# Four-layer cross-attention on one core: in layer 2, values kept in their heads' own columns and multiplied by Wo a tile later, in place of a folded V·Wo

## Chip, cores and metric

The kernel runs on one core of a Trainium2 chip. The metric is the device time of one execution in microseconds (us). Before the change three runs gave 2443.85, 2446.23 and 2447.73 us, a median of 2446.23 us.

## What is computed

The input `x` is [4, 1024, 256] in float32 and passes four attention layers, each against the same context of 77 rows a batch; every layer has 16 heads. The change concerns layer 2. Cut to its core, the reference computes there

```
q = (x @ Wq.T + bq)    k = (ctx @ Wk.T + bk)    v = (ctx @ Wv.T + bv)      # 16 heads of 16 columns
scores = q @ k.T / 4 * attention_weights ; masked to -inf
p   = softmax(scores)                                                      # [4, 16, 1024, 77]
out = (p @ v, heads side by side: [1024, 256]) @ Wo.T + bo
x   = layernorm(x + out) * gamma + beta
```

For a tile of 128 rows of `x` the weights `p` are 16 heads times 77 keys, 1232 numbers a row. The two products after the softmax can be done in either order: `(p @ v) @ Wo`, or `p @ (v @ Wo)` with `v @ Wo` worked out once for each head and batch.

## The kernel before

**Stages.** Layer 0 runs in 16 steps (4 batches of 4 "quads" of heads), then layer 1 in 16 more, then layer 2 and layer 3, each over 32 tiles of 128 rows. Layer 0 takes about the first 900 us, layer 1 ends near 1834, layer 2 has its scores from 1843 to 2097, and layer 3 runs to the end.

**How work is ordered.** The order on each engine is that in which the program issues instructions; every engine works its own queue in order, and semaphores join them. A `step` of layer 0 goes through bursts of score matmuls (line 502). After each burst, `gap` (line 472) and `fill` (line 483) issue pieces of side jobs: a `Job` (line 444) has a number of pieces, a stretch of the step in which they fall due, and, for `fill`, a cost in us (`us=`). All DMAs are issued by SyncE (SP), in program order, and all land through one queue.

**The first quad (0, 0)**, at about 40 to 113 us, has no softmax work yet: 11 bursts of scores for maxima (`Max0`, line 611), each followed by reductions on VectorE (`mpart`, line 650). Its jobs (lines 1588 to 1596) are values of layer 0, contexts, the values, folded values and keys of layer 2, and the statistics of the next batch. Before burst 6 the rows of K reach `qk` by four DMAs (`spread`, line 375); after them come the 13 DMAs that fill `qk` for the next quad.

**Folded values.** `values2` (line 931) makes v turned, with two copies of which each keeps every second head (`hsel2`). `folded2` (line 981) goes through `folded` (line 959) in 24 pieces; each multiplies a head pair's v by its rows of Wo into two PSUM tiles `pu` (128 rows by 256), copies both with ScalarE (line 920) to a staging place, and writes them with DMAs (line 974) to `kept_u[0]` in DRAM, as rows (head, key) of 256. `folded3` does the same later for layer 3, into `kept_u[1]`. `keys2` (line 945) shares the staging places.

**A slot of layer 2** (`slot2`, line 1403) works on several tiles at once. For slot i:

- ScalarE: 16 exponentials, one a head, of tile i-1 (line 1419);
- TensorE: scores of tile i into two PSUM pairs `ps`; VectorE: product with `fside` (line 1431, twice), masking (line 1436), later the maxima `nm` (line 1448, 1452);
- `gap2`: pieces of jobs (the next batch's queries `prep2`, line 1373; the layer norm of the batch before, `norm2`, line 1470);
- TensorE: `po` of tile i-4 (line 1444), ten matmuls over chunks of 128 (head, key) rows, the turned weights `pT` stationary and `U` (128 x 256) moving; VectorE adds it to `x` (line 1458), GpSimd adds `bo`;
- TensorE: the weights of tile i-3 turned in three groups of four, four and two chunks (`turned`, line 1332), each copied by ScalarE (line 1339) into `pT`;
- `gap2` again; then VectorE sums the exponentials of tile i-1 (line 1464, 1465), and GpSimd divides (line 1466).

`load_folded` (line 1354) brings `U` of a batch in two DMAs. The PSUM pool `sm` has three buffers, used in turn by the turned groups, by `prep2` and by nearly every other small product; `pv` has one. After the 32 slots, four more slots without new scores finish the lag, each set ahead of a slot of layer 3 (line 1725, 1772).

Of the kernel before, what the change touches and what calls it, by code (L numbers as in the profile page):

```python
# [17 lines left out]
P = 128  # L18
# [13 lines left out]
def tile_xattn_seq(ctx: ExitStack, tc: tile.TileContext, d: dict, out: bass.AP):  # L32
# [128 lines left out]
    row_tile("be2", "r4", d["L0_xattn_be2"])  # L161
    row_tile("b2", "r5", d["L0_xattn_b2"])

    ctn = work.tile([S, NB - 1, D], F32, name="ctn", tag="hT", bufs=3)
    nc.sync.dma_start(out=ctn, in_=d["ctx_1024"][1:NB].rearrange("b s e -> s b e"))
    load_cols_of(("L2_xattn_bv", 2), ("L2_xattn_bk", 2))
    l2 = {}
    w2s = wpool.tile([P, 3, 2, D], F32, name="w2s", tag="s3")
    for i, key in enumerate(("L2_Wv_t", "L2_Wo_t", "L2_Wk_t")):
        l2[key[3:5]] = w2s[:, i]  # L170
        load_plain(w2s[:, i], d[key])
# [43 lines left out]


    hsel = work.tile([P, HH], F32, name="hsel", tag="hsel", bufs=1)
    hsel2 = work.tile([P, 2], F32, name="hsel2", tag="hsel2", bufs=1)
    hsel4 = work.tile([P, 4], F32, name="hsel4", tag="hsel4", bufs=1)
# [24 lines left out]
    def head_masks():  # L244

        nc.gpsimd.memset(hsel, 1.0)
        nc.gpsimd.affine_select(
            out=hsel, in_=hsel, compare_op=ALU.is_ge, fill=0.0, base=0,
            pattern=[[-DH, HH]], channel_multiplier=1,
        )  # L250
        nc.gpsimd.affine_select(
            out=hsel, in_=hsel, compare_op=ALU.is_ge, fill=0.0, base=DH - 1,
            pattern=[[DH, HH]], channel_multiplier=-1,
        )
        nc.vector.tensor_reduce(
            hsel2, hsel.rearrange("p (r e) -> p e r", e=2), axis=AX.X, op=ALU.add
        )
# [673 lines left out]
    def values2():  # L931

        vb = shared["v2"] = []
        for o in range(2):
            pk = of_contexts(l2["Wv"], o)
            v = work.tile([P, 2, NS], F32, name="v2", tag="hT", bufs=3)
            for e in range(2):
                nc.vector.tensor_scalar(
                    v[:, e, :], pk, cols["L2_xattn_bv"][:, o : o + 1], hsel2[:, e : e + 1],
                    ALU.add, ALU.mult,  # L940
                )
            vb.append(v)
            yield
# [36 lines left out]

    def folded2():

        pairs = []
        for o in range(2):
            for r in (0, 2):
                for e in range(2):
                    h = HH * o + 2 * r + e
                    two = [slice(HP * (r + k), HP * (r + k) + HP) for k in range(2)]
                    pairs.append((
                        slice(h, h + 3, 2), [shared["v2"][o][q, e, :] for q in two],  # L990
                        [l2["Wo"][q, o, :] for q in two],
                    ))
        yield from folded(kept_u[0], pairs, True)

    def heads3(key):
# [25 lines left out]
    def folded3():  # L1021

        two = [slice(0, 64), slice(64, P)]
        yield from folded(
            kept_u[1],
            [
                (slice(2 * f, 2 * f + 2), [shared["wv"][f // 3][r, f % 3, :] for r in two],
                 [l3["wo"][r, f, :] for r in two])
                for f in range(8)
            ],  # L1030
            False,
        )
# [314 lines left out]
    def load2():  # L1347
        l2["Wq"] = wpool.tile([P, 2, D], F32, name="w2q", tag="s3")
        load_plain(l2["Wq"], d["L2_Wq_t"])
        row_tile("bo", "r2", d["L2_xattn_bo"])  # L1350
        row_tile("gamma", "r3", d["L2_xattn_gamma"])
        row_tile("beta", "r4", d["L2_xattn_beta"])

    def load_folded(i, b):

        U = late.tile([P, NC, D], F32, name=f"U{i + 2}", tag="qu")
        rows_of_u = kept_u[i][b].rearrange("h s n -> (h s) n")
        n = P * (NC - 1)
        nc.sync.dma_start(
            out=U[:, 0 : NC - 1, :], in_=rows_of_u[0:n].rearrange("(c p) n -> p c n", p=P)  # L1360
        )
        nc.sync.dma_start(out=U[0:HSIZE, NC - 1, :], in_=rows_of_u[n:HK])
        return U

    def loads2(b):

        shared["u2", b] = load_folded(0, b)
        yield
# [34 lines left out]
    def slot2(i, tiles, at, gap2):  # L1403


        p1, p3, p4 = tiles.get(i - 1), tiles.get(i - 3), tiles.get(i - 4)
        a = None
# [12 lines left out]
        if a:  # L1420
# [81 lines left out]
    def loads3(b):  # L1502

        G = late.tile([P, 2, 8, 2, S], F32, name="G3", tag="gs")
        nc.sync.dma_start(
            out=G.rearrange("p c f e s -> p (c f e) s"),
            in_=kept_g.rearrange("p c f e (b s) -> p (c f e) b s", s=S)[:, :, b, :],
        )
        shared["b3", b] = (G.rearrange("p c f e s -> p c (f e s)"), load_folded(1, b))
        yield  # L1510
# [69 lines left out]
    def jobs0(b, quad):  # L1580
# [222 lines left out]
```

## Time and profile before

| | |
|---|---|
| median of three runs | 2446.23 us (2443.85 to 2447.73) |
| the profiled execution: its own time, its span | 2442.25 us, 2440.5 us |
| mean granted TensorE clock | 0.974 of full speed |
| busy share of the span | TensorE 93%, VectorE 57%, ScalarE 43%, GpSimd 26% |
| first quad: first burst, next quad's first maxima | 39.9 us, 114.8 us |
| layer 2: scores of tile 4, scores of tile 31 | 1870.3 us, 2095.5 us (27 slots of 8.34 us in the mean) |

A row of the profile names line, engine, operation, the written and the read tile (their numbers left out) and the shape as partitions by elements. A float32 matmul is recorded as two instructions, so ten matmuls stand as "x20". Their recorded spans overlap by about 0.16 us, since they are pipelined: the pace of a row is the time between starts. PE is TensorE, PEld its weight loads, DVE is VectorE, ACT ScalarE, POOL GpSimd, SPq the queue of SyncE that issues DMAs.

### The profile page before, as it was taken

What the parts mean: (1) busy time and instruction counts of PE and PEld (TensorE: products, weight loads), DVE (VectorE), ACT (ScalarE), POOL (GpSimd) and SP (SyncE); (2) the same over time, 40 slices, a digit from 0 to 9 for tenths busy, and PEclk for the clock granted to TensorE, in tenths of its full rate; (3) what the DMA queues carried; (4) which work ended last, traced back from release to release, by engine and by line L of the source; (5) the groups of instructions that cost most, each with busy time, mean ns of one, the idle gap of its engine ahead of it and who ended that gap; (6) DMA issues with size and microseconds to landing.
All of it is one profiled execution on the core that took longest, in us unless ns stands there. A gap on an engine that the chain in (4) does not pass through costs nothing.

```text
span 2440.5 us, 40648 instructions
## 1 busy us (share of the span) xinstructions
PE 2279.2 (93%) x16578; PEld 1418.9 (58%) x16578; DVE 1402.0 (57%) x2365; ACT 1040.1 (43%) x1748; POOL 639.8 (26%) x923
## 2 busy tenths in 40 slices
PE   5799989899998999899999999999998999999999
PEld 3443534454454545444556666666655777788887
DVE  4446556555566545664346435454437899767664
ACT  2244444344443344444443444444445677532222
POOL 2011013111131111311152223333332356552222
PEclk9799999999999999999999999999998999999999
DMA  6412021101000000100000100101104334022200
GB/s 176 119 27 93 6 74 40 47 2 19 2 6 15 6 15 1 20 22 5 14 15 5 19 21 15 19 15 19 19 1 166 119 119 134 25 55 55 55 14 18
DMA packets 87139, 98.54 MB, mean 40 GB/s; under 512 B 31222, under 2 KB 77866, under 8 KB 86826
## 3 DMA queue, kind: packets, MB, share of 16 engines
q1 hardware_dynamic: 86954, 95.95, 14.6%
q8 instruction: 131, 2.15, 0.4%
q14 instruction: 54, 0.44, 0.1%
HBM read 57.70 MB, written 20.59 MB: 32 GB/s over the span
## 4 chain that ended last, share of the span: by engine, by line
PE 79%; DVE 10%; ACT 6%; issue 2%; POOL 2%; DMA 1%; SPq 1%; ACTq 0%; DVEq 0%; POOLq 0%
PE ps L51 33%; PE po L51 16%; PE pp L51 6%; PE pv L51 5%; DVE mpart L650 5%; PE ph L51 4%; PE ppv L51 2%; PE psT L1338 2%; PE pvw L51 2%; PE ptx L345 2%; PE pvl L51 1%; PE pk L51 1%; PE pt L591 1%; PE pu L51 1%; PE pm L574 1%
## 5 line engine op out<-in xcount | busy, mean ns | idle before, releaser
L51 PE MATMUL ps<-qk 32*128 32x192 f32 (+8 forms) x5760 | 608.2, 464 | 76.5 <-DVE mpart L650 22.1
L715 ACT ACTIVATE pe<-ps 128x1024 f32<-128x1024 f32 (+2 forms) x384 | 362.9, 951 | 596.6 <-PE ps L51 588.9
L650 DVE TENSOR_REDUCE mpart<-ps 128x2 f32<-128x1024 f32 (+3 forms) x448 | 409.4, 934 | 344.8 <-PE ps L51 344.0
L51 PEld LDWEIGHTS ps<-qk 32*128 32x128 f32 (+1 forms) x5760 | 287.4, 184 | 328.8 <-issue 97.5
L51 PE MATMUL po<-U,pT 128*128 128x256 f32 (+1 forms) x1280 | 291.9, 384 | 7.4 <-DVE x L1458 4.7
L718 POOL TENSOR_SCALAR_AFFINE_SELECT pe<-pe 128x256 f32<-128x256 f32 (+1 forms) x192 | 94.8, 494 | 698.1 <-ACT pe L715 697.1
L51 PEld LDWEIGHTS po<-U,pT 128*128 128x128 f32 (+1 forms) x1280 | 241.1, 192 | 50.1 <-ACT pT L1339 8.0
L1109 DVE TENSOR_REDUCE mrow<-ps 128x4 f32<-128x768 f32 x128 | 122.6, 958 | 142.8 <-PE ps L51 142.4
L1339 ACT COPY pT<-psT 128x512 f32<-128x512 f32 (+1 forms) x192 | 92.0, 518 | 227.9 <-PE psT L1338 227.8
L1184 ACT ACTIVATE pew<-ps 128x768 f32<-128x768 f32 x128 | 103.3, 810 | 173.2 <-PE ps L51 172.7
L1189 POOL TENSOR_SCALAR_AFFINE_SELECT pew<-pew 128x512 f32<-128x512 f32 x128 | 81.3, 635 | 344.1 <-ACT pew L1184 344.1
L51 PE MATMUL pv<-pe,va 128*32 128x512 f32 (+3 forms) x1536 | 159.8, 504 | 0.0
L51 PE MATMUL ps<-G,xT 128*128 128x308 f32 x512 | 143.0, 423 | 0.0
L1419 ACT ACTIVATE s<-s,nm 128x77 f32<-128x77 f32 x512 | 131.3, 354 | 15.9 <-DVE nm L1452 15.9
L51 PE MATMUL ph<-yT,w 128*128 128x256 f32 x512 | 133.7, 398 | 0.8 <-DVE qk L576 0.8
L1551 POOL TENSOR_TENSOR s<-s,den 128x1232 f32<-128x1232 f32 x32 | 71.9, 2248 | 207.8 <-DVE den L1550 184.8
L51 PE MATMUL po<-w,hT 128*128 128x128 f32 (+1 forms) x800 | 124.6, 310 | 0.0
L51 PEld LDWEIGHTS po<-w,hT 128*128 128x128 f32 x800 | 110.0, 193 | 20.4 <-issue 13.8
L51 PEld LDWEIGHTS ph<-yT,w 128*128 128x128 f32 x512 | 94.1, 197 | 38.6 <-issue 24.5
L51 PEld LDWEIGHTS ps<-G,xT 128*128 128x128 f32 x512 | 92.6, 190 | 26.7
L576 DVE TENSOR_TENSOR qk<-pm,qk 128x512 f32<-128x512 f32 x64 | 44.1, 689 | 105.3 <-PE pm L574 105.3
L51 PEld LDWEIGHTS <-identb 128*128 128x128 bf16 x576 | 33.1, 97 | 104.4 <-issue 100.3
(191 smaller groups left out, 3250.6 us busy)
## 6 DMA issues: line engine op xcount, KB each, us to landing
side<-in_fside_t SPq DMA_DIRECT2D x32, 616.0 KB
qk<-st SPq DMA_DIRECT2D x256, 64.0 KB
U<-kept_u SPq DMA_DIRECT2D x8, 1152.0 KB
side<-in_mask_t SPq DMA_DIRECT2D x32, 154.0 KB
G<-kept_g SPq DMA_DIRECT2D x4, 1232.0 KB
x<-in_x SPq DMA_DIRECT2D x8, 512.0 KB
out<-x SPq DMA_DIRECT2D x32, 128.0 KB
kept_u<-st SPq DMA_DIRECT2D x22, 154.0 KB
```

The costliest lines, as they stand in the source:

```text
L51: nc.tensor.matmul(o, lhsT, rhs, start=start, stop=stop, **kw)
L345: nc.tensor.transpose(pt[:, i, :], xn[i][:, c * P : (c + 1) * P], ident)
L650: nc.vector.tensor_reduce(mpart[bl][:, i, 2 * p : 2 * p + 2, ci], ps[:, :, o : o + w], axis=AX.X, op=ALU.max,)
L715: nc.scalar.activation(pp[:n, :, o:512], ps[:n, :, o:512], AF.Exp, scale=SC)
L718: nc.gpsimd.affine_select(out=own, in_=own, compare_op=ALU.is_ge, fill=0.0, base=0, pattern=[[0, 2], [0, k], [1, P]], channel_multiplier=-1,)
L1109: nc.vector.tensor_reduce(mo, ps.rearrange("p j (i n) -> p j i n", i=2)[:, :, :, 0 : P + WIN], axis=AX.X, op=ALU.max, negate=True,)
L1184: nc.scalar.activation(pp[:, :, :, 0 : P + WIN], ps.rearrange("p j (i n) -> p j i n", i=2)[:, :, :, 0 : P + WIN], AF.Exp, scale=SC,)
L1189: nc.gpsimd.affine_select(out=pf[:, :, 0:P], in_=pf[:, :, 0:P], compare_op=ALU.is_ge, fill=0.0, base=0, pattern=[[0, 4], [1, P]], channel_ ...
L1338: nc.tensor.transpose(ps[:, k, :], s[:, P * c : P * c + P], ident)
L1339: nc.scalar.copy(pT[:, 4 * group : 4 * group + n, :], ps[:, 0:n, :])
L1419: nc.scalar.activation(hs, hs, AF.Exp, bias=p1["nm"][:, h : h + 1], scale=SC)
L1551: nc.gpsimd.tensor_tensor(s3, s3, den.unsqueeze(2).to_broadcast([P, H, S]), ALU.mult)
```

## The change

Layer 2's values are no longer folded with Wo. `values2` first writes zeros over a DRAM buffer `kept_v`, then makes v of each batch untransposed (77 x 256, four products), adds the bias row, and writes each half of eight heads by one DMA: head j's row for a key is a row of 128 numbers with v in columns 16j to 16j+15 and zeros elsewhere. `folded2` and `hsel2` are gone. A batch's values come back as 11 chunks `V` of 128 rows by 128 columns, five for the first eight heads and six for the last eight (the fifth and the sixth go with the same chunk of weights), by five DMAs and one memset. In a slot, `V` is stationary and the turned weights move past it (11 matmuls with 128 moving columns), which gives the tile's attention output turned; ScalarE copies it to `oT`; one slot later two matmuls with 256 moving columns multiply it by Wo. The lag goes from four slots to five. The bias row takes the place of `b2`, which is loaded later; Wo is loaded at layer 1 beside Wq.

```diff
-    row_tile("b2", "r5", d["L0_xattn_b2"])
+    row_tile("bv2", "r5", d["L2_xattn_bv"])
...
-    w2s = wpool.tile([P, 3, 2, D], F32, name="w2s", tag="s3")
-    for i, key in enumerate(("L2_Wv_t", "L2_Wo_t", "L2_Wk_t")):
+    w2s = wpool.tile([P, 2, 2, D], F32, name="w2s", tag="s3")
+    for i, key in enumerate(("L2_Wv_t", "L2_Wk_t")):
...
     def load_w2():
+        row_tile("b2", "r5", d["L0_xattn_b2"])
...
     def values2():
-        vb = shared["v2"] = []
-        for o in range(2):
-            pk = of_contexts(l2["Wv"], o)
-            v = work.tile([P, 2, NS], F32, name="v2", tag="hT", bufs=3)
-            for e in range(2):
-                nc.vector.tensor_scalar(
-                    v[:, e, :], pk, cols["L2_xattn_bv"][:, o : o + 1], hsel2[:, e : e + 1],
-                    ALU.add, ALU.mult,
-                )
-            vb.append(v)
-            yield
+        n = NB * 2 * HH * DIAG // P // 8
+        nc.gpsimd.memset(stg[:, 0:n], 0.0)
+        nc.sync.dma_start(
+            out=kept_v.rearrange("b e x -> (b e x)").rearrange("(p k n) -> p k n", p=P, n=n),
+            in_=stg[:, 0:n].unsqueeze(1).to_broadcast([P, 8, n]),
+        )
+        yield
+        for b in range(NB):
+            pk = sm.tile([S, D], F32, name="pk", tag="sm")
+            for c in range(2):
+                mm(pk, ctxT[:, b, c, :], l2["Wv"][:, c, :], start=(c == 0), stop=(c == 1))
+            v = place(3, NS)[:S, 0:D]
+            nc.vector.tensor_tensor(v, pk, rows["bv2"][:S], ALU.add)
+            for e in range(2):
+                to = kept_v[b, e].rearrange("(j x) -> j x", x=DIAG)[:, 0 : S * P]
+                nc.sync.dma_start(
+                    out=to.rearrange("j (s p) -> s j p", p=P)[:, :, 0:DH],
+                    in_=v[:, P * e : P * e + P].rearrange("s (j r) -> s j r", r=DH),
+                )
+            yield
...
-    def folded2():
...
     def load2():
-        l2["Wq"] = wpool.tile([P, 2, D], F32, name="w2q", tag="s3")
-        load_plain(l2["Wq"], d["L2_Wq_t"])
+        w = wpool.tile([P, 2, 2, D], F32, name="w2q", tag="s3")
+        for i, key in enumerate(("L2_Wq_t", "L2_Wo_t")):
+            l2[key[3:5]] = w[:, i]
+            load_plain(w[:, i], d[key])
...
     def loads2(b):
-        shared["u2", b] = load_folded(0, b)
+        V = late.tile([P, NC, D], F32, name="V2", tag="qu").rearrange("p c n -> p (c n)")
+        V = V[:, 0 : (NC + 1) * P].rearrange("p (c n) -> p c n", n=P)
+        lo, hi = [kept_v[b, e, 0:HALF].rearrange("(r n) -> r n", n=P) for e in range(2)]
+        k = HH * S % P
+        nc.gpsimd.memset(V[:, 4:6, :], 0.0)
...
+        shared["v2", b] = V
         yield
...
     def slot2(i, tiles, at, gap2):
-        p1, p3, p4 = tiles.get(i - 1), tiles.get(i - 3), tiles.get(i - 4)
+        p1, p3, p4, p5 = (tiles.get(i - k) for k in (1, 3, 4, 5))
...
+        if p5:
+            xt = xs[p5["b"]][:, p5["t"], :]
+            po = pvp.tile([P, D], F32, name="po2", tag="pv")
+            for o in range(2):
+                mm(po, p5["oT"][:, o, :], l2["Wo"][:, o, :], start=(o == 0), stop=(o == 1))
+            del tiles[i - 5]
         if p4:
-            U = shared["u2", p4["b"]]
-            xt = xs[p4["b"]][:, p4["t"], :]
-            po = pvp.tile([P, D], F32, name="po2", tag="pv")
-            for c in range(NC):
+            V = shared["v2", p4["b"]]
+            pv = sm.tile([P, 2, P], F32, name="pvT", tag="sm")
+            for k in range(NC + 1):
+                o, c = (0, k) if k < 5 else (1, k - 1)
                 r = slice(0, rows_in(c))
-                mm(po, p4["pT"][r, c, :], U[r, c, :], start=(c == 0), stop=(c == NC - 1))
-            del tiles[i - 4]
+                mm(pv[:, o, :], V[r, k, :], p4["pT"][r, c, :], start=k in (0, 5), stop=k in (4, NC))
+            oT = p4["oT"] = late.tile([P, 2, P], F32, name="oT", tag="oT")
+            nc.scalar.copy(oT, pv)
...
-        if p4:
+        if p5:
             nc.vector.tensor_tensor(xt, po, xt, ALU.add)
             nc.gpsimd.tensor_tensor(xt, xt, rows["bo"], ALU.add)
...
-            j.append(Job(values2(), 2, 0.1, 0.2, us=1.0))
-            j.append(Job(folded2(), 24, 0.2, 1.0, us=0.85))
+            j.append(Job(values2(), 5, 0.3, 0.9, us=0.85))
...
-            j.append(Job(norm2(NB - 1), 16, 0.1, 1.0))
+            j.append(Job(norm2(NB - 1), 16, 0.15, 1.0))
...
-    run(slots(slot3, 2, jobs3, slots(slot2, 4, jobs2)))
+    run(slots(slot3, 2, jobs3, slots(slot2, 5, jobs2)))
```

More of the change, by code (lines that the diff above doesn't have):

```diff
@@ L161, in tile_xattn_seq @@
     row_tile("be2", "r4", d["L0_xattn_be2"])
-    row_tile("b2", "r5", d["L0_xattn_b2"])
+    row_tile("bv2", "r5", d["L2_xattn_bv"])
     ctn = work.tile([S, NB - 1, D], F32, name="ctn", tag="hT", bufs=3)
     nc.sync.dma_start(out=ctn, in_=d["ctx_1024"][1:NB].rearrange("b s e -> s b e"))
-    load_cols_of(("L2_xattn_bv", 2), ("L2_xattn_bk", 2))
+    load_cols_of(("L2_xattn_bk", 2))
     l2 = {}
-    w2s = wpool.tile([P, 3, 2, D], F32, name="w2s", tag="s3")
-    for i, key in enumerate(("L2_Wv_t", "L2_Wo_t", "L2_Wk_t")):
+    w2s = wpool.tile([P, 2, 2, D], F32, name="w2s", tag="s3")
+    for i, key in enumerate(("L2_Wv_t", "L2_Wk_t")):
         l2[key[3:5]] = w2s[:, i]
@@ L217, in tile_xattn_seq @@
     hsel = work.tile([P, HH], F32, name="hsel", tag="hsel", bufs=1)
-    hsel2 = work.tile([P, 2], F32, name="hsel2", tag="hsel2", bufs=1)
     hsel4 = work.tile([P, 4], F32, name="hsel4", tag="hsel4", bufs=1)
@@ L253, in head_masks @@
             pattern=[[DH, HH]], channel_multiplier=-1,
-        )
-        nc.vector.tensor_reduce(
-            hsel2, hsel.rearrange("p (r e) -> p e r", e=2), axis=AX.X, op=ALU.add
         )
@@ L900, in tile_xattn_seq @@
     kept_g = dram.tile([P, 2, 8, 2, NS], F32, name="kept_g")
-    kept_u = [dram.tile([NB, H, S, D], F32, name=f"kept_u{i}") for i in range(2)]
+    kept_u = dram.tile([NB, H, S, D], F32, name="kept_u")
+    HALF, DIAG = HH * S * P, S * P + DH
+    kept_v = dram.tile([NB, 2, HH * DIAG], F32, name="kept_v")
     stg = wpool.tile([P, 1024], F32, name="stg", tag="s7")
@@ L979, in folded @@
                 yield
-    def folded2():
-        pairs = []
-        for o in range(2):
-            for r in (0, 2):
-                for e in range(2):
[L987 to L993, printed above, removed]
     def heads3(key):
@@ L1024, in folded3 @@
         yield from folded(
-            kept_u[1],
+            kept_u,
             [
@@ L1352, in load2, with load_folded @@
         row_tile("beta", "r4", d["L2_xattn_beta"])
-    def load_folded(i, b):
-        U = late.tile([P, NC, D], F32, name=f"U{i + 2}", tag="qu")
-        rows_of_u = kept_u[i][b].rearrange("h s n -> (h s) n")
+    def load_folded(b):
+        U = late.tile([P, NC, D], F32, name="U3", tag="qu")
+        rows_of_u = kept_u[b].rearrange("h s n -> (h s) n")
         n = P * (NC - 1)
@@ L1365, in loads2 @@
     def loads2(b):
-        shared["u2", b] = load_folded(0, b)
+        V = late.tile([P, NC, D], F32, name="V2", tag="qu").rearrange("p c n -> p (c n)")
[3 more added lines that the diff above has]
+        nc.gpsimd.memset(V[:, 4:6, :], 0.0)
+        nc.sync.dma_start(
+            out=V[:, 0:4, :], in_=lo[0 : 4 * P].rearrange("(c p) n -> p c n", p=P)
+        )
+        nc.sync.dma_start(out=V[0:k, 4, :], in_=lo[4 * P :])
+        nc.sync.dma_start(out=V[k:P, 5, :], in_=hi[0 : P - k])
+        nc.sync.dma_start(
+            out=V[:, 6:10, :], in_=hi[P - k : 5 * P - k].rearrange("(c p) n -> p c n", p=P)
+        )
+        nc.sync.dma_start(out=V[0:HSIZE, 10, :], in_=hi[5 * P - k :])
+        shared["v2", b] = V
         yield
@@ L1508, in loads3 @@
         )
-        shared["b3", b] = (G.rearrange("p c f e s -> p c (f e s)"), load_folded(1, b))
+        shared["b3", b] = (G.rearrange("p c f e s -> p c (f e s)"), load_folded(b))
         yield
```

## The prediction

> **What bounds the kernel now.** I read the busy time by stage first, because the page's shares mix stages with different limits. Columns: window, length, busy us (instructions) of PE, PEld, DVE, ACT, POOL, then granted clock, DMA share, GB/s.
>
> ```profile
> 70.00:80.00 10.00, 3.36 (x18) 1.47 (x16) 0.60 (x1) 0.65 (x2) 0.00 (x0) 0.73 0.44 104
> 80.00:90.00 10.00, 5.33 (x20) 3.60 (x20) 5.45 (x8) 1.97 (x7) 0.00 (x0) 0.50 0.42 124
> ```
>
> ```profile
> 1870.00:1946.00 76.00, 75.61 (x385) 56.21 (x386) 64.71 (x88) 51.86 (x178) 27.46 (x27) 1.00 0.34 112
> 1946.00:1975.00 29.00, 27.74 (x156) 22.46 (x156) 27.18 (x36) 25.35 (x85) 22.81 (x30) 1.00 0.31 101
> 1975.00:2012.00 37.00, 36.70 (x184) 26.40 (x182) 32.73 (x49) 23.50 (x81) 15.04 (x15) 1.00 0.38 128
> 2012.00:2034.00 22.00, 21.01 (x119) 17.03 (x120) 20.86 (x29) 18.15 (x61) 15.79 (x21) 1.00 0.29 92
> 2034.00:2103.00 69.00, 60.62 (x320) 47.94 (x316) 64.88 (x108) 48.23 (x164) 42.48 (x51) 0.95 0.37 111
> ```
>
> Two places matter. In the first quad no engine is busy between 70 and 90 us; something else is waited for. In layer 2 TensorE is full at first, but VectorE stands at 85% to 95% throughout: work taken from TensorE is worth only what VectorE leaves. The chain of waits (start, length, what) says what is late in the first quad:
>
> ```profile
> 71.85 0.48 SPq L974
> 72.33 0.06 issue
> 72.44 0.31 SPq L974
> 72.75 0.05 issue
> 72.80 4.03 DMA kept_u<-st
> ...
> 79.86 4.05 DMA kept_k<-st
> 84.06 0.38 ACT st L920
> 84.48 1.06 PE pu L51 x2
> ```
>
> SP first issues the next quad's `qk` DMAs (62 to 72 us); `folded2`'s writes stand behind them, its staging places stay taken, ScalarE cannot copy `pu`, and TensorE stands. The group of `pu` has the size:
>
> ```profile
> L51 PE MATMUL pu<-w2s,v 32*128 32x256 f32 x96 | 26.7, 530 | 15.0 <-ACT st L920 12.4 <-DVE wfd L1058 1.6 <-ACT stg L920 0.9
> ```
>
> So 26.7 us busy and 15.0 us of TensorE idle hang on `folded2`, in a quad of 75 us (39.9 to 114.8).
>
> **First quad, part by part.** *Removed:* 96 `pu` records, 48 ScalarE copies of 0.37 us, the `kept_u` writes of layer 2, and the turned values. *Added:* a zero fill, 16 records of 77 x 256 (four of this shape take 1.02 us, row `pvc`: 4 us in all), four VectorE additions of 0.42 us, eight DMAs.
>
> Up to the K rows' arrival: the chain holds 2.1 us of turned values and about 5.5 us of `pu` and copies between 45 and 61 us. VectorE's reductions, two of 1.1 us a burst, cover part, so I take 5 us: K lands at 58.5 in place of 63.5.
>
> From there to the end of the quad six bursts remain. VectorE's work in them: reductions 4 x 2.36 + 2 x 2.13 = 13.7 (rows of `mpart`, 1.22 and 1.11 each); statistics 6 x 0.55 = 3.3; values 4 x 0.42 = 1.7; `va` 2 x 0.42 = 0.8; keys 8 x 0.58 = 4.6; the rest (`qk`, `wfd`, `mrow`) 1.7. That is 25.8 us. TensorE's share is smaller: per burst 1.14 us of scores at full clock and 1 to 4 us of side products. Scores of the next burst need the buffers that the reductions free, so they run under VectorE's side work of 1 to 2.3 us: I add 3 us for bubbles and half-clock stretches. The next quad's first maxima come at 58.5 + 0.6 + 25.8 + 3 = 87.9, against 114.8: **27 us less**; I use 26.
>
> What could eat this. (a) The zero fill, 2.53 MB: between 20 and 30 us the engines moved 368 GB/s, between 0 and 10 us 249, so 7 to 10 us. It waits only for a memset that GpSimd reaches near 28 us, and SP issues it right after the first Q rows, near 40 us, when DMA is nearly idle (share 0.04 between 40 and 50). It is done by 50, before the K rows need the queue at about 55: 0 us; were it late, up to 10. (b) Eight DMAs of 616 pieces of 64 bytes. No row shows a DRAM write of 64 bytes. SP took 0.3 us for a `kept_u` issue and 2.92 us for the issue that stood behind a DMA of 1024 pieces of 4 bytes: 2.4 to 23 us of SP in all. I take 1 us each: behind the 4096 pieces of 308 bytes of `G` the next issue took 4.46 us, 1.1 ns a piece, 0.7 us for 616, and 0.3 for the issue. SP has these 8 us: the next quad's rows stand ahead of them, and behind them are only key writes and the next weights. The end at 23 us would put the writes at 71 to 94 us and delay the last keys, whose places they free: 5 to 8 us. [...]
>
> **Layer 2, TensorE.** Paces, from the timeline (start, length, row):
>
> ```profile
> 1888.99 4.59 PE L51 MATMUL po<-U,pT 128*128 128x256 f32 x20
> 1893.42 1.26 PE L1338 MATMUL psT<-ident,s 128*128 128x128 f32 x10
> 1894.60 1.31 PE L51 MATMUL ps<-kb,qT 64*128 64x308 f32 x8
> ```
>
> ```profile
> 703.07 1.95 PE L51 MATMUL po<-w,hT 128*128 128x128 f32 x16
> ```
>
> `po` takes 4.42 us for 20 records, 221 ns each. 128 moving columns against 128 x 128 weights take 117 ns (layer 0's feed-forward: 16 records, the next work starting 1.88 us later). New: 22 x 0.117 = 2.6 us, and 4 x 0.221 = 0.9 us with Wo: 3.5 in place of 4.4, **0.94 us less a tile**. [...]
>
> **What of it counts.** A slot without jobs takes TensorE 6.85 us (1887.8 to 1894.6). VectorE's own work, start to start: products 1.48, mask 1.51, maxima 1.5, sum into `x` 0.33, exponentials' sum 1.45 and 0.17, gaps: 6.6 us. So such a slot gains 0.25 us, not 0.94; with a copy of `xT` (0.69) about 0.35 to 0.7; with two blocks of `prep2` (10.6 us on TensorE) the full 0.94. By slots: tile 4 loses `po` for `pv` (4.4 to 2.6): 1.8; tiles 5 to 7: 0.75; tiles 8 to 12: 3.2; tiles 16 to 20: 3.5. Tiles 21 to 31 mostly run along VectorE (64.9 of 69 us) and lose only waits for `po`, which now comes first in the slot: 1. ScalarE gains one copy of 128 x 256 a slot, 0.39 us (row `pT`, 389 ns). It is hidden, ScalarE being at 50 of 76 us, except where `norm2` fills it (1946 to 1975, 2012 to 2034): about 6 slots, 2.4 lost. The lag: four `po` of 4.4 after the last scores become four `pv` of 2.6 and five `po` of 0.9, where layer 3 keeps TensorE full: 2.9 gained. Sum 1.8 + 0.75 + 3.2 + 3.5 + 1 - 2.4 + 2.9 = **10.7 us less**; I use 10. Bounds: 0 (VectorE decides everywhere) to 30 (0.94 x 32).
>
> The new `V` loads move 0.7 MB a batch where `U` took 1.2; their memset on GpSimd waits for the last use of the buffer, within the slot in which `U`'s DMA waited: nothing. `bv2`, the later `b2` and Wo's other place are loads without a reader nearby: nothing.
>
> **Sum.** 2442.25 - 26 - 10 = 2406 against the profiled execution. The median of the runs lies 4 us above it, so I predict **2410 us**.
>
> **Rivals.**
> - *Layer 2 gives nothing* (20%): VectorE, or ScalarE with 32 x 0.39 us more, sets every slot. For it: VectorE at 85% to 95%. Against it: 113 us in which TensorE is full. 2446 - 26 = 2420, 2414 to 2424.
> - *The first quad gives little* (12%): zero fill, 64-byte writes or a half-clock TensorE (0.50 between 80 and 90 us) refill the 26 us up to 10. For it: SP was late there before. 2446 - 10 - 10 = 2426, up to 2434.
> - *All 0.94 us count* and the quad ends at 84.5 without bubbles (8%): 2446 - 30 - 30 = 2386.
> - *Slower* (7%): the copy of `oT` stands behind ScalarE's 16 exponentials, and `pv` holds one of three `sm` buffers; the third turned group needs that buffer, and the next scores stand behind it. If that closed a loop within one slot it would be 4.1 (exponentials) + 0.39 + 0.25 + 0.74 (scores) + 4.5 (VectorE to the maxima) = 10 us a slot, 1.6 above the mean of 8.34: +53 over 32 slots, -26 from the quad, 2473. It decides from 0.8 us a slot. Against it: these exponentials need the maxima of the slot before, so the loop spans two slots, 5 us each.
>
> That the change doesn't do what it says is excluded by the changed kernel's program order: `folded2` is gone, 22 and 4 records stand in each slot.
>
> **How the numbers follow.** Forecast 53%, by itself 2398 to 2420; rivals 20, 12, 8, 7. The range 2396 to 2434 leaves out the last two and little else, and takes in the bounds of the writes (8) and of layer 2. A measurement of this kernel can tell about 0.2%, 5 us. Faster by more: 0.91, within: 0.02, slower: 0.07.
>
> **What would show it.** The next quad's first maxima near 88 us; `pv` of 22 records in 2.6 us; slots without jobs at about 6.6 us, VectorE over 90% of layer 2; layer 3's part after the first five slots unchanged. Wrong if TensorE waits for the `sm` buffer or SP is late after 71 us.

## The result and the profile after

The changed kernel takes **2411.66 us** (median of 4 runs, 2409.19 to 2417.36), the kernel before 2445.04 us in the same job (4 runs, 2442.32 to 2447.73): ratio 0.9864, 95% interval 0.9843 to 0.9885. That is 33.4 us less. The forecast was 2410 us, with a range of 2396 to 2434. The profiled execution of the changed kernel took 2409.19 us with a span of 2407.5 us, the one before 2442.25 and 2440.5.

The first quad, by stage, in the changed kernel (columns as before: window, length, busy us of PE, PEld, DVE, ACT, POOL, then granted clock, DMA share, GB/s):

```profile
70.00:80.00 10.00, 9.59 (x44) 4.37 (x42) 9.90 (x19) 0.00 (x0) 0.00 (x0) 1.00 0.51 100
80.00:90.00 10.00, 7.06 (x23) 3.23 (x24) 8.68 (x18) 1.02 (x1) 1.92 (x2) 0.70 0.34 75
```

Between 70 and 80 us no engine was busy for more than 3.36 of 10 us before; between 80 and 90 TensorE and VectorE were busy for about half (5.33 and 5.45), so the prediction's "no engine is busy" fits the first ten us only. Now VectorE is busy for 9.90 and 8.68 us. The chain of waits of the changed kernel over the same time (start, length, what) has neither SP nor a DMA in it; it runs from one VectorE instruction to the next:

```profile
71.00 2.26 DVE mpart L646 x2
73.26 0.34 DVE st L303
73.63 0.18 DVE mv L304
73.81 0.48 DVE st L959
74.30 0.51 DVE stg L959
74.80 0.33 DVE st L944
75.13 2.26 DVE mpart L646 x2
...
83.86 1.03 DVE mpart L646
85.03 2.93 PE ps L51 x8
```

The next quad's first maxima start at 87.07 us in place of 114.80, 27.7 earlier. The next marker, that quad's second group of scores on TensorE, starts at 90.92 in place of 116.06: 25.1 earlier. The first marker overstates the gain, because before the change those maxima stood on VectorE behind two instructions for layer 2's keys, which waited for writes of `kept_u`:

```profile
112.88 0.60 DVE L951 TENSOR_SCALAR st<-pk,c_L_xattn_bk,hsel 128x308 f32<-128x308 f32 x1 [3.21 <-DMA kept_u<-st]
114.29 0.60 DVE L951 TENSOR_SCALAR st<-pk,c_L_xattn_bk,hsel 128x308 f32<-128x308 f32 x1 [0.81 <-DMA kept_u<-stg]
```

They began 1.4 us after the score records ahead of them had ended (113.42); in the changed kernel they begin 0.9 us before the last of these records ends (87.96). The records themselves end 25.5 us earlier. The granted clock was 0.50 around them in both kernels (110.0 to 113.4 us, 84.0 to 88.0 us), so 25 us is what the quad gives.

Layer 2's TensorE rows, from the timeline of the changed kernel:

```profile
1854.29 1.31 PE L51 MATMUL ps<-kb,qT 64*128 64x308 f32 x8
1855.52 1.13 PE L51 MATMUL po<-w2q,oT 128*128 128x256 f32 x4
1856.49 2.62 PE L51 MATMUL pvT<-pT,V 128*128 128x128 f32 x22
1858.95 1.26 PE L1332 MATMUL psT<-ident,s 128*128 128x128 f32 x10
```

From start to start `po` takes 0.97 us and `pvT` 2.46: 3.43 where the old `po` took 4.42, so about 1.0 us less a tile on TensorE.

What it is worth shows in the stretches of tiles. They are cut where VectorE begins a tile's first product (`s<-ps,side`), because VectorE is the busiest engine of the changed kernel there (231.5 of 246.8 us); the starts of the scores run ahead of it by 0.8 to 7.2 us and mislead. Stage windows of the kernel before, tiles 0 to 13, 13 to 17, 17 to 21, 21 to 24 and 24 to 31, and then the same tiles of the changed kernel:

```profile
1844.20:1946.70 102.50, 93.48 (x450) 65.20 (x448) 90.46 (x119) 66.66 (x231) 32.24 (x32) 0.92 0.38 126
1946.70:1977.60 30.90, 29.64 (x168) 23.75 (x165) 29.00 (x38) 27.25 (x94) 25.28 (x32) 1.00 0.31 103
1977.60:2012.90 35.30, 35.00 (x174) 25.28 (x172) 31.10 (x49) 21.70 (x72) 12.59 (x14) 1.00 0.38 126
2012.90:2035.40 22.50, 21.51 (x121) 17.22 (x118) 21.59 (x28) 18.75 (x64) 17.03 (x21) 1.00 0.33 106
2035.40:2097.90 62.50, 54.73 (x287) 43.26 (x286) 58.52 (x102) 42.50 (x146) 36.14 (x45) 0.95 0.39 117
```

```profile
1819.40:1913.80 94.40, 83.69 (x500) 59.58 (x500) 89.09 (x118) 70.46 (x240) 31.97 (x33) 0.91 0.38 123
1913.80:1946.80 33.00, 28.45 (x191) 22.97 (x188) 30.62 (x37) 28.55 (x98) 25.70 (x32) 0.90 0.29 96
1946.80:1978.30 31.50, 31.03 (x197) 23.20 (x197) 30.65 (x48) 23.56 (x77) 12.53 (x14) 1.00 0.38 121
1978.30:2003.30 25.00, 20.76 (x136) 16.66 (x132) 22.79 (x28) 20.33 (x68) 19.53 (x25) 0.86 0.30 96
2003.30:2066.20 62.90, 52.09 (x332) 43.38 (x331) 58.34 (x102) 44.20 (x153) 34.03 (x41) 0.89 0.39 116
```

Two stretches are shorter, by 8.1 and 3.8 us; the two in which `norm2` runs are longer, by 2.2 and 2.4 between the exact starts; the last is 0.4 longer. In sum 253.7 us become 246.8. VectorE's busy time hardly moves: 230.7 and 231.5. So its idle time went from 23.0 to 15.3 us, and that is the whole gain: TensorE lost 18.3 us of busy time (234.4 to 216.0) and could only give what VectorE had been waiting for. (By its rows it saved about 30, of which less shows because the granted clock over the five stretches is lower: 0.95 before, 0.91 after.)

These lengths repeat: executions of other kernels with the same layer 2 code gave 253.7 again for the old one (run 1 below), and 246.6, 246.3 and 246.4 for the new one (runs 2, 10 and 11). Differences of a few us, which the runs' times can't tell, are read from them. One stretch has to be taken out first: from tile 3's first product to tile 4's. In the kernel before, the changed kernel and runs 1, 2, 4, 7, 8, 10 and 11 it takes 7.3 to 7.4 us, with a mean granted clock of 0.77; in runs 3, 9 and 12 it takes 6.3, 6.1 and 6.1 us at a clock of 1.00. The records of the queries (`prep2`) that fall in it, in the changed kernel and then in run 3:

```profile
1842.13 3.52 PE L51 MATMUL pp<-xT,w2q 128*128 128x512 f32 x4
```

```profile
1847.05 1.98 PE L51 MATMUL pp<-xT,w2q 128*128 128x512 f32 x4
```

Run 3's edit takes effect only behind this stretch, so these 1.1 us are the clock's and not the edit's.

### The profile page after: what moved, and what is told of

Same layout as the page of the kernel before. It is cut to its first block, busy times and chain, and to the rows that moved or that the text cites. A ratio compares the mean times of both kernels' runs of the same rounds, so it can differ in the third digit from the quotient of the medians.

```text
span 2407.5 us, 40744 instructions
## 1 busy us (share of the span) xinstructions
PE 2241.1 (93%) x16682; PEld 1393.0 (58%) x16682; DVE 1400.6 (58%) x2364; ACT 1035.8 (43%) x1732; POOL 641.3 (27%) x928
## 4 chain that ended last, share of the span: by engine, by line
PE 78%; DVE 12%; ACT 6%; issue 2%; POOL 1%; DMA 1%; SPq 0%; ACTq 0%; DVEq 0%; POOLq 0%
PE ps L51 34%; PE po L51 13%; PE pp L51 6%; DVE mpart L646 5%; PE pv L51 5%; PE ph L51 4%; PE ppv L51 2%; PE psT L1332 2%; PE pvw L51 2%; PE ptx L341 2%; PE pvT L51 1%; PE pvl L51 1%; PE pt L587 1%; PE pk L51 1%; PE pm L570 1%
## 5 line engine op out<-in xcount | busy, mean ns | idle before, releaser
L51 PE MATMUL po<-U,pT 128*128 128x256 f32 (+1 forms) x640 | 143.7, 380 | 0.2
L51 PEld LDWEIGHTS po<-U,pT 128*128 128x128 f32 (+1 forms) x640 | 119.2, 190 | 15.5 <-ACT pT L1333 0.6
L51 PEld LDWEIGHTS ph<-yT,w 128*128 128x128 f32 x512 | 93.9, 196 | 38.8 <-issue 24.6
L1332 PE MATMUL psT<-ident,s 128*128 128x128 f32 x640 | 93.1, 274 | 14.6 <-ACT oT L1464 10.6
```

Of the source, the lines that this page charges most:

```text
L51: nc.tensor.matmul(o, lhsT, rhs, start=start, stop=stop, **kw)
L1332: nc.tensor.transpose(ps[:, k, :], s[:, P * c : P * c + P], ident)
```

## The experiments

Medians stand beside those of the kernel before in the same job; ratios are to it, with 95% intervals. "Tile 0 to 31" is the length just explained, in the profiled execution.

**Runs 1 and 2: each half alone.** Run 1 has the changed kernel's first quad and the old layer 2, run 2 the reverse. The buffer that the other half would have filled is filled from a weight instead, in layer 0's last batch:

```
+            if (b, quad) == (3, 0):
+                nc.sync.dma_start(out=kept_w..., in_=ffw[1][:, 0, 0:n].unsqueeze(1).to_broadcast([P, 22, n]))
```

> The changed kernel's first quad (no folding of Wo for layer 2, zero fill, padded value rows) with the old kernel's layer 2, which reads a buffer of layer 2's old shape that a DMA fills with other numbers from layer 0's batch 3 on: layer 2's values are left out. Theory (two independent gains): the next quad's first maxima come near 87, layer 2 begins 25 us earlier than in the kernel before and runs at its old pace; time 25 us under the kernel before, ratio 0.990 (0.988 to 0.992). Rival (the quad's gain is eaten later unless layer 2 changes too): the marker at 87 holds but the end is less than 15 us earlier, ratio above 0.994.

> The old kernel's first quad, folding for layer 2 included though nothing reads it, with the changed kernel's layer 2, whose value rows are filled with other numbers by a DMA in layer 0's batch 3: layer 2's values are left out. Theory: first maxima of the next quad near 114.8 as before, layer 2 shorter by 8 us (6 to 10), tiles 13 to 17 and 21 to 24 slower by 2 and 3 us; time 8 us under the kernel before, ratio 0.9967 (0.9955 to 0.9978). Rival (layer 2 gives nothing, the whole gain is the first quad's): within 2 us of the kernel before. Rival (all 0.94 us a tile count): 25 to 30 us less.

Run 1: 2419.80 us against 2444.89, ratio 0.9902 (0.9888 to 0.9915): 25.1 us less (21 to 27); next quad's first maxima at 86.8, tile 0 to 31 in 253.7. In its profiled execution, the slowest of its four (2425.23 us), layer 2 begins 17.7 us earlier than before and not the expected 25 (1826.5, 1844.2); the 25.1 rests on the medians. Run 2: 2437.14 against 2444.89, ratio 0.9969 (0.9960 to 0.9978): 7.8 us less (5 to 10), tile 0 to 31 in 246.6. The sum, 32.9, is the whole change's 33.4 within its uncertainty. Two separate gains of 25 and 8 us: that one half eats or carries more than about 7 us of the other is out.

**Run 3: a bank of its own for the turned result.** The prediction's slower rival, a copy of `oT` behind ScalarE's exponentials that holds an `sm` buffer, is in the changed kernel's trace. At tile 14 the third turned group waits for it on TensorE:

```profile
1928.61 0.69 PE L1332 MATMUL psT<-ident,s 128*128 128x128 f32 x2 [4.12 <-ACT oT L1464]
1929.23 2.42 PE L51 MATMUL ps<-kb,qT 64*128 64x308 f32 x8
```

and VectorE's next product then waits 1.53 us for those scores:

```profile
1930.68 0.80 DVE L1442 TENSOR_TENSOR s<-ps,side 128x616 f32<-128x616 f32 x1 [1.53 <-PE ps L51]
```

The scores take 2.42 us here and 1.31 at full clock: the granted clock fell to 0.50 within TensorE's wait. Window of the changed kernel:

```profile
1927.20:1934.00 6.80, 5.39 (x17) 3.53 (x18) 4.97 (x7) 6.80 (x23) 5.82 (x10) 0.50 0.10 37
```

So at least 0.6 of the 1.53 us are the clock's: the product starts 1.45 us after the scores here, and 0.84 us after them at full clock (at tile 4, 1845.58 and 1846.42). The page counts 10.6 us of such waiting of `psT`. Run 3 puts `pvT` beside `po`:

```
+        if p5 or p4:
+            both = pvp.tile([P, 2 * D], F32, name="both", tag="pv")
-            po = pvp.tile([P, D], F32, name="po2", tag="pv")
+            po = both[:, 0:D]
-            pv = sm.tile([P, 2, P], F32, name="pvT", tag="sm")
+            pv = both[:, D:].rearrange("p (o n) -> p o n", o=2)
```

> The changed kernel with the turned result of layer 2 beside po in the one bank of the pv pool instead of one of the three sm buffers; nothing is left out. Theory (the copy of oT behind ScalarE's exponentials holds an sm buffer, and in the norm2 slots the third turned group waits for it): no more idle time of psT ended by the copy of oT (14.6 us in the changed kernel's page, 10.6 by oT), tiles 13 to 17 from 31.6 to about 30, tiles 21 to 24 from 24.6 to about 22.5, end 3 to 5 us under the changed kernel, ratio to before 0.984 to 0.986. Rival (ScalarE's own queue sets these slots, the buffer is only where it shows): the wait moves to the next scores or the maxima and the time stays within 1 us of the changed kernel.

Measured: 2410.21 us, ratio 0.9858 (0.9845 to 0.9872). No `psT` waits for `oT` any more, but tile 0 to 31 is 244.5, 2.3 us less, and of the two `norm2` stretches only 0.2 and 0.05 us went (33.1 to 32.9, 25.0 to 25.0). At the same tile stands, in run 3:

```profile
1929.38 1.28 DVE L1473 TENSOR_SCALAR nm<-nm 128x16 f32<-128x16 f32 x1
...
1931.99 0.42 DVE L1479 TENSOR_TENSOR x<-both,x 128x256 f32<-128x256 f32 x1 [1.33 <-ACT oT L1466]
```

The wait moved: the sum into `x` reads the tile that now also holds the turned result, and stands behind ScalarE's copy of it. The theory, 3 to 5 us in the `norm2` stretches, fell; the rival was nearer. Of the 2.3 us, 1.1 are the clock's at tile 3 (above), so in this kernel the buffer alone costs about 1.2 us of the whole layer.

**Run 4: `norm2`'s first activation later.** One more step ahead of it (the job has 17 pieces in place of 16):

```
         nc.gpsimd.tensor_scalar(away, away, -1.0, None, ALU.mult)
+        yield
```

> The changed kernel with one more step between the inverse deviation of norm2 on GpSimd and its first activation on ScalarE, so that ScalarE need not wait 3.1 us for GpSimd with the exponentials and the copy of oT queued behind it; nothing is left out. Theory: that wait of 3.1 us goes in the three norm2 stretches of layer 2 and the tiles 13 to 17 and 21 to 24 get about 1 us shorter each; 2 to 3 us under the changed kernel in all. Rival (the eight norm2 activations themselves fill ScalarE, the wait only moves): within 1 us of the changed kernel. A cost is possible too: the last norm2 pieces come half a slot later, 0 to 1 us.

Measured: 2411.75 us, ratio 0.9870 (0.9857 to 0.9884); tile 0 to 31 in 246.4. ScalarE's waiting for GpSimd in layer 2 only falls from 12.8 to 10.9 us, and nothing is gained: the theory fell.

**Runs 5 and 6: VectorE relieved.** The line `nc.vector.copy_predicated(sv, mk, ...)` is taken out of both kernels.

> The kernel before without the masking of layer 2's scores on VectorE (32 instructions of 1.5 us, 48 us in all; the mask is left out of the result). Theory (VectorE's rows set layer 2's pace in both kernels and TensorE is close behind in the one before): from the first product of tile 0 to that of tile 31, 253.7 us before, comes down only to TensorE's own busy time, about 240; the end 10 to 15 us under the kernel before, ratio 0.994 to 0.996. Rival (VectorE is not the limit): within 3 us of the kernel before.

> The changed kernel without the masking of layer 2's scores (the mask is left out of the result). Theory (VectorE is what eats most of the 0.94 us a tile): with 48 us of VectorE's work gone, TensorE's saving shows nearly whole: tile 0 to 31 from 246.8 to 215 to 224 us, 2382 to 2390 us in all; the gap to the kernel before without its mask is 40 to 48 us where the two with masks lie 33 apart, so layer 2's part is 15 to 23 instead of 8. Rival (the saving is lost on TensorE or by the sm buffer, not to VectorE): the gap stays at 33, within 3 us. Rival (ScalarE with 5.8 us of its own a slot takes over): tile 0 to 31 stays over 228.

Measured: 2431.82 us without the mask in the kernel before, ratio 0.9950 (0.9937 to 0.9962); 2390.59 in the changed one, ratio 0.9778 (0.9765 to 0.9792), both beside 2444.34. Tile 0 to 31 of run 5 and of run 6, as stage windows:

```profile
1845.80:2085.50 239.70, 227.90 (x1185) 170.60 (x1182) 184.74 (x300) 176.34 (x603) 123.27 (x140) 0.98 0.39 126
```

```profile
1818.80:2043.20 224.40, 206.56 (x1348) 160.06 (x1345) 182.82 (x298) 186.00 (x630) 123.53 (x142) 0.96 0.40 126
```

Taking 48 us of work from VectorE gives the old kernel 14.0 us, because TensorE is close behind (227.9 of 239.7), and the new one 22.4. The gap between the kernels grows from 33.4 to 41.2 us, and layer 2's part, tile 0 to 31, from 6.9 to 15.3. So of the about 30 us that TensorE's rows save, 6.9 counted beside VectorE's masking and 15.3 without it: the masking hid 8.4, and the rest is held by something else. The expected 215 to 224 us was missed by 0.4 and the 2390 by 0.6; the rival that ScalarE takes over (over 228) was not reached.

**Run 7: another form of the small instruction.** In both `norm2` stretches the changed kernel has rows such as these, VectorE's clamp and scale of the maxima and GpSimd's division of the exponentials:

```profile
1925.97 1.28 DVE L1471 TENSOR_SCALAR nm<-nm 128x16 f32<-128x16 f32 x1
```

```profile
1924.91 2.25 POOL L1485 TENSOR_TENSOR s<-s,den 128x1232 f32<-128x1232 f32 x1
```

The median of the 32 clamps is 0.17 us. This one takes 1.28 and ends at 1927.25, 0.1 us behind the division (1927.16). In five of the 32 tiles it takes 1.06 to 1.40, 5.4 us more in all; in the kernel before such waits add up to 3.2 us.

```
-            nc.vector.tensor_scalar(nm, nm, 0.1 * NEG, -SC, ALU.max, ALU.mult)
+            nc.vector.scalar_tensor_tensor(nm, nm, 0.1 * NEG, minus_sc, ALU.max, ALU.mult)
```

> The changed kernel with the clamp and scale of the maxima (128 x 16, 0.17 us as a rule, but up to 1.4 us in five of the 32 tiles, each time until GpSimd's division of 2.25 us ends) as an instruction with a second tensor operand in place of the one with two scalars; nothing is left out. Theory (a lock between this form of VectorE instruction and GpSimd's division lengthens the norm2 stretches by 1.7 and 1.1 us of their 2.2 and 2.4): all 32 at 0.2 us or less, 13 to 17 by VectorE's products from 33.1 to about 31.5, 21 to 24 from 25.0 to about 24, end 3 to 5 us under the changed kernel. Rival (it waits for something else that ends with the division, such as the exponentials' sum): the delay moves to the next instruction, within 1 us of the changed kernel.

Measured: 2410.24 us, ratio 0.9864 (0.9850 to 0.9877), tile 0 to 31 in 246.9. The other form waits in the same way, up to 1.32 us with a median of 0.17:

```profile
1927.32 1.23 DVE L1473 SCALAR_TENSOR_TENSOR nm<-nm,minus_sc 128x16 f32<-128x16 f32 x1
```

It ends at 1928.55, and GpSimd's division in this run at 1928.52. The theory that this form would escape fell. The rows show what the instruction ends with, not what holds it.

**Run 8: the bank again, with the sum ahead of the copy.** As run 3, but the sum into `x` stands ahead of the copy of `oT`, which follows the copies of `pT`:

```
-            nc.scalar.copy(oT, pv)
...
         if p5:
             nc.vector.tensor_tensor(xt, po, xt, ALU.add)
             nc.gpsimd.tensor_tensor(xt, xt, rows["bo"], ALU.add)
+        if p4:
+            nc.scalar.copy(oT, pv)
```

> The changed kernel with the turned result beside po in the pv bank, as in the run of that name, but the sum into x now stands ahead of the copy of oT, and this copy behind the three copies of pT; nothing is left out. In the first form the sum into x waited for the copy of oT (1.33 us at tile 14), a wait that the shared bank had added. Theory (VectorE's idle time of 15.3 us in tiles 0 to 31 is what is left to gain, and half of it hangs on the copy of oT): idle 15.3 to about 8 to 11, layer 2 shorter by 4 to 7 us than in the changed kernel, 2405 to 2408 in all. Rival (the remaining idle time is VectorE's wait for ScalarE's exponentials): idle stays at 12 as in the first form, 2 to 3 us under the changed kernel.

Measured: 2409.83 us, ratio 0.9858 (0.9845 to 0.9872); tile 0 to 31 in 244.8 with 15.9 us of VectorE idle. The theory fell: the idle time did not go. 3.8 us of it stand in front of the sum into `x`, which now waits for TensorE (`both`). But the `norm2` stretches are shorter, 31.8 and 24.6 us in place of 33.1 and 25.0. From first product to first product, tiles 14 and 22 took 7.69 and 7.79 us in the kernel before, 9.30 and 9.41 in the changed one, 9.20 and 9.30 with the bank alone (run 3), and take 7.69 and 7.80 here. So the 1.6 us that each of these two tiles lost come from the place of the copy of `oT` in ScalarE's order together with its buffer. Of what they give back, tile 23 loses 1.2 again (8.00 to 9.24).

**Run 9: no small instruction at all.** The factor goes into the queries' activation, the reduction negates, and the clamp is left out:

```
-                nm, sv.rearrange("p (h k) -> p h k", k=S), axis=AX.X, op=ALU.max
+                nm, sv.rearrange("p (h k) -> p h k", k=S), axis=AX.X, op=ALU.max, negate=True
-            nc.vector.tensor_scalar(nm, nm, 0.1 * NEG, -SC, ALU.max, ALU.mult)
-                    bias=cols["L2_xattn_bq"][:, o : o + 1], scale=1.0,
+                    bias=bq2[:, o : o + 1], scale=SC,
```

> The changed kernel with layer 2's factor 0.25 applied where the queries leave TensorE's buffer (the same activation as before), the maxima negated by the reduction that finds them, and so without the 32 small clamp-and-scale instructions on VectorE; left out is the clamp, which only rows without any key need. Theory (VectorE sets layer 2, and these instructions cost it 32 x 0.175 us and 5.5 us of waiting until GpSimd's division ends, 11 us in all): tile 0 to 31 by VectorE's products from 246.8 to 237 to 241, end 6 to 10 us under the changed kernel, 2402 to 2406. Rival (in the norm2 stretches ScalarE or the sm buffer sets the pace, as the second operand's form showed, where the small instruction still waited): 2 to 4 us. Rival (nothing, TensorE is next at once): within 1 us.

Measured: 2403.38 us against 2442.88, ratio 0.9838 (0.9823 to 0.9852); tile 0 to 31 in 241.6. VectorE's busy time fell by 10.2 us (231.5 to 221.3), the stretch by 5.2; idle time rose from 15.3 to 20.3. Of the 5.2, 1.1 are the clock's at tile 3, so some 4 of 10 us counted in layer 2. The median lies in the expected 2402 to 2406 us; the expected 237 to 241 was missed by 0.6. Where the rest went shows in the `norm2` stretches: they hardly moved (33.1 to 32.8, 25.0 to 24.5) though the small instruction and its wait were gone from them. At tile 14 of run 9 TensorE stands for the same reason as in the changed kernel:

```profile
1925.47 0.69 PE L1333 MATMUL psT<-ident,s 128*128 128x128 f32 x2 [3.92 <-ACT oT L1465]
```

and what stands ahead of that copy on ScalarE is this:

```profile
1919.59 0.60 ACT L1499 ACTIVATE x<-x,away,rs 128x256 f32<-128x256 f32 x1 [2.94 <-POOL away L1496]
1920.09 4.09 ACT L1431 ACTIVATE s<-s,nm 128x77 f32<-128x77 f32 x16
1924.09 1.08 ACT L1499 ACTIVATE x<-x,away,rs 128x256 f32<-128x256 f32 x2
1925.07 0.34 ACT L1465 COPY oT<-pvT 128x256 f32<-128x256 f32 x1
```

`norm2`'s first activation waits 2.94 us for GpSimd (`away`), and the exponentials and the copy stand behind it.

**Run 10: the writes twice.** The zero fill and each value-row write are issued a second time, into a buffer that nothing reads:

```
-                nc.sync.dma_start(out=to..., in_=v...)
+                for kept in (kept_v, kept_z):
+                    nc.sync.dma_start(out=to..., in_=v...)
```

> The changed kernel with the zero fill and the eight value-row writes issued twice each, the second time into a buffer that nothing reads: 2.5 MB more of zeros near 41 us and eight more DMAs of 616 pieces of 64 bytes. Nothing is left out. Theory (both are hidden): the fill is done near 60 us at worst, the next quad's first maxima stay at 87 us within 1 us, the end within 1.5 us of the changed kernel (ratio to before 0.985 to 0.988). Rival (the fill's price is only just hidden, so that twice as much pushes the K rows issued at 57 us): the maxima 3 to 8 us later and the end as much. Rival (SP's issue time of the value rows counts, 0.45 us each): 3 to 4 us later.

Measured: 2412.99 us against 2442.88, ratio 0.9881 (0.9864 to 0.9899), too wide to tell a few us. The marks say it: first maxima at 87.64 in place of 87.07, the next scores at 91.55 in place of 90.92. Stage windows of the changed kernel (first) and of run 10:

```profile
50.00:60.00 10.00, 8.08 (x60) 5.85 (x57) 7.23 (x15) 0.00 (x0) 0.00 (x0) 0.83 0.13 20
```

```profile
50.00:60.00 10.00, 8.13 (x50) 5.87 (x52) 6.71 (x16) 0.00 (x0) 0.00 (x0) 0.74 0.88 247
```

The second fill occupies the engines for another ten microseconds (DMA share 0.88 in place of 0.13), and the quad's end moves by 0.6 us. Even that is not all the writes': run 7, which has the changed kernel's first quad and nearly run 10's granted clock (0.50, 0.52 and 1.00 from 55, 60 and 65 us on; run 10 has 0.50, 0.50 and 0.99), shows 87.34 and 91.25. In the change itself the fill and the 64-byte writes are hidden.

**Run 11: less of VectorE's work in the first quad.** The next batch's statistics move to the second quad:

```
-        if quad == 0 and b + 1 < NB:
-            j.append(Job(stats0(b + 1), 8, 0.3 if b == 0 else 0.0, 1.0))
+        if quad == (0 if b else 1) and b + 1 < NB:
+            j.append(Job(stats0(b + 1), 8, 0.0, 1.0))
```

> The changed kernel with the statistics of the next batch (bn_stats and bn_aggr, 0.42 and 0.18 us a tile, six to eight of them on VectorE) moved from the first quad to the second. Nothing is left out. Theory (VectorE sets the first quad from 60 us on): the next quad's first maxima from 87.1 to 83 to 84.5, and as the second quad is TensorE's, the end 2 to 4 us under the changed kernel. Rival (TensorE at half clock, or SP, sets the end of the first quad): the maxima stay within 1 us of 87. Rival (the second quad is VectorE's as well): the maxima come earlier and the end does not.

Measured: 2411.13 us, ratio 0.9863 (0.9849 to 0.9878). The first maxima come at 86.06, only 1.0 earlier, and the second maxima at 91.90, against 92.02. Run 11, stage windows and the scores after the maxima:

```profile
60.00:70.00 10.00, 10.00 (x42) 6.28 (x39) 4.97 (x8) 0.00 (x0) 0.00 (x0) 0.60 0.35 58
70.00:80.00 10.00, 9.78 (x50) 4.90 (x48) 10.00 (x14) 0.00 (x0) 0.00 (x0) 1.00 0.49 95
```

```profile
89.95 2.01 PE L51 MATMUL ps<-qk 32*128 32x461 f32 x8
```

From 70 us on VectorE is full, as the theory has it, and that part is shorter: from the burst at 68.0 to the maxima 19.1 us in the changed kernel, 16.3 here (from 69.75). But between 60 and 70 us TensorE is busy all the time at a granted clock of 0.60 (1.00 in the changed kernel), and the burst from 62.8 to 69.75 takes 1.6 us longer than the changed kernel's from 62.6 to 68.0. That is not the edit's doing. Run 8, whose first quad is the changed kernel's, has the same clock there:

```profile
60.00:70.00 10.00, 10.00 (x42) 6.30 (x38) 5.84 (x11) 0.00 (x0) 0.00 (x0) 0.61 0.35 57
```

Its first maxima come at 88.72 and its second at 93.30. Against it run 11 is 2.7 us earlier at the first, as the theory has it (2.6 to 4.1), and 1.4 at the second: behind the first maxima run 11's eight scores take 2.01 us, where those of run 8 and of the changed kernel take 1.10. So VectorE sets the quad from 70 us on, as forecast, and about half of what was taken from it came back as time of a slower TensorE. The end cannot tell 1.4 us, and the forecast 2 to 4 us are not seen in it. The clock differs between executions of the same code, and marks are to be compared at the same clock.

**Run 12: the two edits that helped.** Runs 3 and 9 together.

> Both edits of the changed kernel that took time from layer 2: the scale in the queries (241.6 us from tile 0 to 31 by VectorE's products, in place of 246.8; the clamp for rows without any key is left out) and the turned result in the pv bank (244.5). Theory (the idle time that the first left on VectorE in the norm2 stretches, 5.3 and 4.2 us, hangs on the copy of oT that holds an sm buffer, so that the second is worth more now than its 2.3 us alone): tile 0 to 31 in 236 to 239, end 3 to 5 us under the kernel with the scale alone, 2398 to 2401. Rival (ScalarE's 10 us a slot set these stretches, with or without the buffer): tile 0 to 31 in 239.5 to 241.5, end 0 to 2 us under it.

Measured: 2401.52 us against 2443.91, ratio 0.9832 (0.9814 to 0.9851); tile 0 to 31 in 239.4. Of the kernels that keep the mask it is the fastest, by a margin over run 9 that the runs' times cannot tell. The stage is 2.3 us shorter than in run 9 and lies between the two ranges (236 to 239, 239.5 to 241.5). The bank alone also gave 2.3, but 1.1 of that were the clock's at tile 3, and 0.2 stood in the `norm2` stretches. Here tile 3 is as short as in run 9, and 1.7 stand in the `norm2` stretches (32.8 to 31.4 and 24.5 to 24.1). So the buffer is worth more once VectorE is relieved, as the theory has it, but less than forecast. In the first stretch the granted clock is also higher, 0.95 in place of 0.90, and this run does not separate the two. The 10 us a slot of the rival are in no row: in the first `norm2` stretch of the changed kernel ScalarE is busy for 28.55 of 33.00 us, 7.1 a slot. VectorE's waits in layer 2 (what waits, for what: us in total, times, longest) in the kernel before and in run 12:

```profile
DVE s L1431 <- PE ps L51: 11.5, 7, 6.8
DVE x L1458 <- PE po L51: 6.7, 7, 1.9
```

```profile
DVE x L1478 <- ACT oT L1467: 10.1, 7, 2.8
DVE s L1443 <- PE ps L51: 9.0, 2, 6.8
```

In the kernel before VectorE waits for TensorE; in run 12, apart from one wait of 6.8 us ahead of tile 0, most of its waiting is for ScalarE's copy of `oT`.

## Why the prediction was right, point by point

- **Both parts and their sum.** 26 + 10 us were forecast; 25.1 and 7.8 were measured, each alone. The first quad's part held by its mechanism. Within layer 2 two terms are wrong by 2.4 and 2.2 us with opposite signs (below); that they cancel is luck.
- **First quad.** 87.9 us was forecast for the first maxima, 87.07 measured; eight other executions of the same first quad have 86.3 to 88.7. The step to the K rows was a little large: from the first burst to their issue 15.5 us in place of 19.8 (41.51 to 57.02, 39.92 to 59.71), 4.3 and not 5, and as the first burst came 1.6 later here, the sixth begins at 59.98 and not at the forecast's 59.1. From there to the maxima VectorE is busy for 25.2 us (25.8 forecast) and idle for 1.9 (3 forecast).
- **Zero fill, value rows.** Costed at 0 and hidden: run 10. SP took 0.42 us (median of eight) for a value-row issue, not 1.
- **TensorE's pace.** 2.6 + 0.9 us were forecast, 2.46 + 0.97 measured. A record with 128 moving columns takes 112 ns in `pvT`, one with 256 took 221 in the old `po`.
- **What of it counts, by VectorE's products.** Tile 4: 1.9 us (1.8 forecast). Tiles 5 to 7: 0.7 (0.75), 6.7 us each, as forecast for slots without jobs. Tiles 8 to 12: 5.6 (3.2): *mis-sized*; the slots of tiles 8, 11 and 12, with most of `prep2`'s work, gave 1.7, 1.4 and 1.8 us each, not 0.94. Tiles 17 to 20: 3.8 (3.5 forecast for 16 to 20). Tiles 21 to 31: 1 forecast beside `norm2`'s loss; tiles 24 to 30 gave nothing (0.4 lost here, 0.1 in runs 2, 10 and 11). `norm2`: 2.4 lost was forecast, and 2.2 + 2.4 = 4.6 measured: *mis-sized*, by counting the added copy of 0.39 us alone and not what stands behind it. Lag and layer 3: 2.9 forecast, 1.3 measured, which is not firm: from tile 31's first product to the end four executions of the changed layers (the changed kernel, runs 2, 10 and 11) took 341.3 to 343.0 us, two of the old ones (the kernel before, run 1) 342.6 and 343.3.
- **Why `norm2` costs 4.6.** By VectorE's rows the first stretch's 2.2 us are 0.5 of idle time and 1.7 of the small instruction's wait for GpSimd's division, the second's 2.4 are 1.3 and 1.1. But run 9 took the wait away and the stretches stayed within 0.5 us: idle time came in its place. What is shown is where most of the loss begins: 1.6 us each at tiles 14 and 22, and both go when the copy of `oT` has its own bank and stands behind the copies of `pT` (run 8). The rest stands at tiles 15 and 23; with the bank and without the small instruction (run 12) the stretches are 31.4 and 24.1 us, against 30.9 and 22.6 before the change. For this rest two causes stand side by side. One is ScalarE's order of exponentials, `norm2`'s activations and the copy of `oT`. The other is the granted clock: 1.00 in both stretches before, 0.90 and 0.86 after. Where the first stretch has a clock of 0.95 (runs 8 and 12) it takes 31.8 and 31.4 us; in the changed kernel and the seven other runs with its mask and a clock of 0.90 it takes 32.8 to 33.1. No run took `norm2`'s activations off ScalarE or held the clock, so the rest stays open.
- **The slower rival** was real as a mechanism: `psT` waits 10.6 us for `oT`. "Wrong if TensorE waits for the `sm` buffer" was too strong: TensorE waits, and since VectorE sets the pace only about 1.2 us of that counted in the changed kernel (run 3), 2.3 beside run 9's edit (run 12). The rival that layer 2 gives nothing is out by run 2, and that all of 0.94 us counts by runs 2, 5 and 6.

## What to carry to other kernels

Before counting on work taken from one engine, read by stage the idle time of the engine behind it: here VectorE's 23.0 us, of which 7.7 were won, out of about 30 saved on TensorE. Cut stages at the starts of the engine that sets the pace, since the starts of the one ahead of it run early (here by up to 7.2 us) and make one stretch look good and the next bad. When a wait is taken away, look for the instruction that now waits in its place before counting the gain. And before a gain of a few us is given to an edit, compare the granted clock of the same stretch in an execution of the same code: here 1.1 us at one tile were the clock's, and so was most of what seemed to be lost in run 11.

## What the runs showed of the hardware that was not expected

- A VectorE instruction on 128 x 16 elements in SBUF took up to 1.40 us in place of 0.17 when GpSimd's 128 x 1232 division was under way, and ended 0.1 us behind it; the form with a second tensor did the same (1.23 and 1.19 us in the first `norm2` stretch, 1.32 at most). Reductions that ran into the same five divisions kept their 1.44 us, and masks that started within other divisions took 1.60 to 1.62.
- TensorE's granted clock in the first quad differs between executions of the same code: between 55 and 60 us 0.67 in the changed kernel and run 1, 0.50 in run 3; between 60 and 70 us 1.00 in the changed kernel, 0.61 in run 8. The next quad's first maxima came at 87.07 us in the changed kernel and at 88.72 in run 8.
- A write of 616 pieces of 64 bytes to DRAM cost SP 0.31 to 0.58 us an issue, about as much as a `V` load (0.33 to 0.50 in 19 of 20, 1.24 in one).
